# Gate operations issued one by one behind the evacuations of up, and unread products of TensorE ahead of the first loads

## The chip, the cores and the metric

The kernel runs on one NeuronCore of a Trainium2 chip. The metric is the device time of one execution in microseconds (us), as a median of several runs. The engines are TensorE (PE, with its weight loads listed apart as PEld), VectorE (DVE), ScalarE (ACT), GpSimd (POOL) and SyncE (SP, which only issues DMAs here). Each engine works through a queue of its own in order.

## The reference

A block of cross attention and a quantised feed-forward block, over 4096 tokens of 512 features.

```python
x = x + _L0_xattn_ref(_layernorm(x, axis=-1), ctx_1024, L0_xattn_Wq, L0_xattn_Wkv)
x = x + _L0_ffn_ref(_layernorm(x, axis=-1), L0_ffn_w_gate, L0_ffn_w_up, L0_ffn_w_down)
```

The attention is `softmax(hWq (cWk)^T / sqrt(512)) cWv` with 128 context rows for each of the two batches. In the feed-forward block every activation tensor is rounded to 16-bit integers with one scale for the whole tensor:

```python
x = act_qdq(x)
up = act_qdq(x @ lpbq_dequant(w_up).T)
gate = act_qdq(x @ lpbq_dequant(w_gate).T)
sig = fixed_qdq_u16(jax.nn.sigmoid(gate))
gate = act_qdq(gate * sig)
o = act_qdq(gate * up)
return o @ lpbq_dequant(w_down).T
```

`act_qdq` needs the largest magnitude of its tensor before the first element can be rounded. So the stages of the kernel stand one behind the other.

## The kernel before, in words

There are four stages, each over eight groups of 512 tokens.

**Attention** (0 to about 157 us of the profiled execution). The context `c_sb` and the matrix `wq_sb` are turned by TensorE (lines 400 and 408) into PSUM tiles of two banks, which come from a pool `ps_t` with two buffers. VectorE copies the turned context to `cT` (line 401), ScalarE copies the turned matrix to `wqT` (line 409). From `cT` come the keys (`pk`, line 417, copied to `kT` by ScalarE in line 424), from `wqT` and `kT` the product `pg` (line 431), which becomes `kTG` (line 438, then line 445 on VectorE, which takes a mean `pm` off). Then each group g has its scores `sc` (line 351), softmax (`e`, line 364), turned weights (`pe`, copied to `eT` in line 466), values `po` (line 478, added to x in line 479), the second layernorm (lines 497 to 508) and the turn of `h` into `hT`. `front(g)` works ahead on the transposes of x (line 311) and its statistics (line 338 on VectorE; for group 1 lines 321, 324, 326 and 333 with ScalarE). In between, the gate's weights are dequantised, turned and split (`split_weights`, lines 180 to 215). The stage ends in one number, the largest `h` (`a_h`), and TensorE has nothing of the gate stage to do before it is known.

**Gate** (to 434.9 us), **up** (to about 701 us), **down** (to the end). In the up stage (loop from line 857) step c makes half of a tile of up: sixteen products q and eight products e of TensorE (lines 621 and 627), ScalarE's evacuation of q (line 878) and VectorE's subtraction of e (line 879). q and e have two buffers each, so the products of step c + 2 wait for the evacuation of step c. Beside this, ScalarE makes the gelu of one gate tile in three operations of 128x2048 elements: line 769 to integers, line 772 the sigmoid, line 773 the sigmoid as 16-bit integers. They are called G1, G2 and G3 below. It also makes |up| for a bound (line 819, called b below). VectorE makes p = gi * sq (line 812), the bound's product (line 820) and the largest |up| (line 180). SP loads gate tiles (line 755) and stores up (line 893) and p (line 813).

The order on each engine is not that of the source. A scheduler places each instruction by its own estimate of when its inputs are ready. `in_order(a, b)` forces b behind a on one engine; `advance(steps, n)` runs n steps of a generator.

Of the kernel before, what the change touches and what calls it, by code (L numbers as in the profile page):

```python
# [49 lines left out]
F32 = mybir.dt.float32  # L50
# [6 lines left out]
AF = mybir.ActivationFunctionType  # L57
# [6 lines left out]
P = 128  # L64
# [12 lines left out]
def tile_xattn_ffn(  # L77
# [11 lines left out]
    nc = tc.nc  # L89
    B, S, D = x.shape  # L90
# [5 lines left out]
    NQ = 4  # L96
    NK = NF // NQ
    TG = 512
# [11 lines left out]
    ident = const.tile([P, P], F32, name="ident")  # L110
# [8 lines left out]
    order = [(t, k) for t in reversed(range(NG)) for k in range(NK)]  # L119
    gate_d = dram.tile([NG * NK, P, NQ, TG], F32, name="gate_d")  # L120
    NH = 2 * NG * NK
# [47 lines left out]
    def in_order(*instructions):  # L169

        for one, behind in zip(instructions, instructions[1:]):
            tc.add_manual_dep(
                behind.ins,
                one.ins.name,
                mybir.DependencyInfo(mybir.DependencyClass.NoSync, mybir.DependencyReason.DATA),
                reason="order of issue",
            )
# [63 lines left out]
    def advance(steps, n):  # L241
        for _ in range(n):
            next(steps, None)
# [29 lines left out]
    with ExitStack() as c0:  # L273
# [3 lines left out]
        with ExitStack() as c1:  # L277
# [5 lines left out]
            ps_s = c1.enter_context(tc.tile_pool(name="ps_s", bufs=2, space=PSUM))  # L283
# [91 lines left out]
            with tc.tile_pool(name="prep0", bufs=1, side="right") as p0:  # L375
# [16 lines left out]
                xts[1] = load_x(1)  # L392
                advance(its[1], 1)

                cT = p0.tile([P, ND, B * KL], F32, name="cT")
                pt = two_banks("ct")
                pt4 = pt.rearrange("p (c b k) -> p c b k", c=ND, b=B)
                for b in range(B):
                    for c in range(ND):
                        nc.tensor.transpose(pt4[:, c, b, :], c_sb[:, b, ts(c, P)], ident)  # L400
                nc.vector.tensor_copy(cT.rearrange("p c k -> p (c k)"), pt)
                wqT = p0.tile([P, ND, D], F32, name="wqT")
                for m in range(0, ND, 2):
                    pt = two_banks(f"wqt_{m}")
                    pt4 = pt.rearrange("p (c m k) -> p c m k", c=ND, m=2)
                    for i in range(2):
                        for c in range(ND):
                            nc.tensor.transpose(pt4[:, c, i, :], wq_sb[:, m + i, ts(c, P)], ident)
                    nc.scalar.copy(wqT[:, :, ts(m // 2, 2 * P)], pt.rearrange("p (c k) -> p c k", c=ND))
                first = front(0)  # L410
                advance(its[0], 3)
# [330 lines left out]
    with ExitStack() as c3:  # L742
# [10 lines left out]
        def load_gate(j, queue=nc.sync):  # L753
            gt = gp2.tile([P, NQ, TG], F32, tag="gt", name=f"gt_{j}")
            queue.dma_start(out=gt, in_=gate_d[j])
            return gt
# [5 lines left out]
        s_g16 = const.tile([P, 1], F32, name="s_g16")  # L762
        nc.vector.tensor_scalar(s_g16, s_g, 1.0 / 65536.0, None, ALU.mult)

        def gelu_like(pool, gt, shape, name, behind=None):

            sq = pool.tile([P] + shape, U16, tag="sq", name=f"sq_{name}")
            gi = pool.tile([P] + shape, I16, tag="gi", name=f"gi_{name}")
            begun = nc.scalar.activation(gi, gt, AF.Copy, scale=r_g)
            if behind is not None:  # L770
                in_order(behind, begun)
            nc.scalar.activation(gt, gi, AF.Sigmoid, scale=s_g)
            nc.scalar.activation(sq, gt, AF.Copy, scale=65536.0)
            return gi, sq


        gi, sq = gelu_like(const, top_g, [1], "top")
# [16 lines left out]

        wd, ready, made_p = [], [], []

        def next_gelu(behind):

            j = len(ready)
            if j < len(order):  # L800
                ready.append(gelu_like(wk3, gts.pop(0), [NQ, TG], j, behind))
                if j + 2 < len(order):
                    gts.append(load_gate(j + 2))

        def next_p():
            j = len(made_p)
# [45 lines left out]
        LAST = len(order) - 1  # L852


        more_gelu = (1, NH // 4 + 1, 3 * NH // 8 + 1, 5 * NH // 8 + 1)
        more_p = (NH // 3 + 1, NH // 2 + 3)
        for j, (t, k) in enumerate(order):
            if k == 0:
                parts = groups.pop(t)
                if t + 1 < NG and t > 0:  # L860
                    groups[t - 1] = load_group(t - 1)
                if t == 0:
                    first_wd = homes[1].tile([P, 3, ND, TG], F32R, tag="parts", name="first_wd")
                    first_wd = first_wd.rearrange("p s c (k d) -> p (s c k d)", k=1).rearrange(
                        "p (f s d) -> p f s d", f=NE, s=3
                    )
                    load_down(range(NE), slice(0, 2))
            u4 = tiles_u[j % NK]
            for h in range(2):
                c = 2 * j + h  # L870
                both = slice(2 * h, 2 * h + 2)
                wu2 = [wu[NQ * k + 2 * h + i] for i in range(2)]
                if c + 1 < NH:
                    q = ps_m.tile([P, 2, TG], F32, tag="q", name=f"q_u{c}")
                    e = ps_m.tile([P, 2, TG], F32, tag="e", name=f"e_u{c}")
                    for i in range(2):
                        project(wu2[i], parts, q[:, i, :], e[:, i, :])
                    evacuated = nc.scalar.activation(u4[:, both, :], q, AF.Copy, scale=1.0 + 1.0 / BASE)  # L878
                    less = nc.vector.tensor_tensor(u4[:, both, :], u4[:, both, :], e, ALU.subtract)  # L879
                    if c + 2 == NH:  # L880
                        in_order(row_known, less)
                else:
                    for i in range(2):
                        v = u4[:, 2 + i, :]
                        q = ps_m.tile([P, 2, TG], F32, tag="q", name=f"q_u{c}_{i}")[:, 0, :]
                        e = ps_m.tile([P, 2, TG], F32, tag="e", name=f"e_u{c}_{i}")[:, 0, :]
                        last_product = project(wu2[i], parts, q, e)
                        nc.scalar.activation(v, q, AF.Copy, scale=1.0 + 1.0 / BASE)
                        nc.vector.tensor_tensor(v, v, e, ALU.subtract)
                        abs_max(umax[:, LAST + 1 + i : LAST + 2 + i], v)  # L890
                if t == 0 and k == 0 and h == 1:
                    load_down(range(NE, NE + NQ), slice(0, 2))
                stored = nc.sync.dma_start(out=up_d[c], in_=u4[:, both, :])
                if h == 0 or c in more_gelu:

                    next_gelu(evacuated if c > 3 else None)
                if h == 0 or c in more_p:
                    next_p()
                pi = kept_p[j % NK]
                if c + 3 < NH:  # L900
                    bound(c, u4[:, both, :], pi[:, both, :])
                elif c + 3 == NH:
                    with tc.high_priority():
                        bound(c, u4[:, both, :], pi[:, both, :])
                        row_known, (ub, pb) = fetch_best()
            if j < LAST:
                abs_max(umax[:, j : j + 1], u4, AX.XY)
            else:
                abs_max(umax[:, j : j + 1], u4[:, :2, :], AX.XY)
# [329 lines left out]
```

## Time and profile before

| | us |
|---|---|
| median of 3 runs | 981.71 (978.31 to 982.92) |
| the profiled execution, its own time | 981.48 |
| its span on the core | 979.7 |
| TensorE busy | 947.5 |
| VectorE busy | 812.5 |
| ScalarE busy | 548.7 |
| first product of the gate stage starts at | 159.49 |
| first product of the up stage starts at | 434.87 |
| first product of the down stage starts at | 711.95 |

The times in the rows below are counted from the start of the span. A row of the timeline is: start, duration, engine, line, operation, output<-input, shapes, count, and in brackets the idle time before it with what ended it. A plain fp32 product of the attention stage, and an unread one, is recorded twice, so sixteen products `sc` stand there as x32. Transposes, and the products of the other three stages, are recorded once. TensorE's clock is given in tenths of full speed, or as a fraction in the table of stretches.

### The profile page before, as it was taken

Reading aid. Unit: us, or ns where it says so; the run is one execution under the profiler, and the core shown is the slowest. Engines: PE = TensorE matmul, PEld = TensorE weight load, DVE = VectorE, ACT = ScalarE, POOL = GpSimd, SP = SyncE. Lnnn points to the kernel's source line nnn. Section 1 sums busy time; section 2 is a strip of 40 time slices with the busy share of each in tenths; the row PEclk is TensorE's granted clock in tenths of the full one; section 3 lists DMA queues with packets and bytes.
Section 4 is the critical chain, followed back from the end, with each engine's and each line's share of the span. In section 5 each row is a group of like instructions: output and inputs, shape, how many; then the busy total and the mean of one; then the engine's idle time right before and its main releaser. Section 6 shows DMA issues by size and latency. Waiting matters only on the chain. (4 is left out here: it accounts for less than half of the span.)

```text
span 979.7 us, 11777 instructions
## 1 busy us (share of the span) xinstructions
PE 947.5 (97%) x4356; PEld 763.4 (78%) x4356; DVE 812.5 (83%) x1013; ACT 548.7 (56%) x668; POOL 77.9 (8%) x62
## 2 busy tenths in 40 slices
PE   6998889999999999999999999999989999999998
PEld 6775656888888888877888888877668888888886
DVE  4979779899899998537988989879799999878882
ACT  3477689323323323229999999795455445353531
POOL 0101111000000000000000000000101221222221
PEclk9999899999999999999999999999999999999999
DMA  9675545967878855897988989979785677656710
GB/s 359 247 280 199 178 178 236 414 266 302 322 311 313 321 194 174 279 409 251 370 315 306 403 285 374 379 270 377 292 319 177 210 256 256 211 152 230 259 64 32
DMA packets 103595, 263.72 MB, mean 269 GB/s; under 512 B 6064, under 2 KB 46000, under 8 KB 94832
## 3 DMA queue, kind: packets, MB, share of 16 engines
q1 hardware_dynamic: 102496, 259.02, 71.7%
q0 software_dynamic: 512, 2.88, 0.9%
q10 hardware_dynamic: 528, 1.05, 0.3%
q8 instruction: 34, 0.56, 0.2%
q14 instruction: 25, 0.20, 0.1%
HBM read 136.05 MB, written 126.88 MB: 268 GB/s over the span
## 5 line engine op out<-in xcount | busy, mean ns | idle before, releaser
L621 PE MATMUL q_g<-parts_g,wg 128*128 128x512 f32 x768 | 193.1, 391 | 0.9 <-ACT parts_g L644 0.9
L621 PEld LDWEIGHTS q_g<-parts_g,wg 128*128 128x128 f32 x768 | 143.4, 188 | 31.2 <-ACT parts_g L644 2.0
L712 ACT ACTIVATE g<-q_g 128x512 f32<-128x512 f32 x96 | 57.3, 598 | 166.0 <-PE q_g L621 155.5
L621 PE MATMUL q_u<-parts_u,wu 128*128 128x512 f32 x576 | 142.7, 390 | 2.6 <-ACT u L878 2.6
L621 PEld LDWEIGHTS q_u<-parts_u,wu 128*128 128x128 f32 x576 | 107.9, 188 | 26.1 <-ACT u L878 3.7
L1040 PE MATMUL yq<-wd,o_parts 128*128 128x512 f32 x512 | 121.4, 389 | 0.5 <-ACT o_parts L1029 0.5
L1040 PEld LDWEIGHTS yq<-wd,o_parts 128*128 128x128 f32 x512 | 96.0, 188 | 20.9 <-ACT o_parts L1029 0.9
L627 PE MATMUL e_g<-parts_g,wg 128*128 128x512 f32 x384 | 103.3, 390 | 0.0
L713 DVE CUSTOM_DVE_ANT_0 g<-g,e_g 128x512 f32<-128x512 f32 x96 | 65.0, 682 | 36.6 <-PE e_g L627 33.4
L627 PEld LDWEIGHTS e_g<-parts_g,wg 128*128 128x128 f32 x384 | 72.0, 188 | 15.1
L1053 ACT ACTIVATE yqs<-yq,q_o 128x512 f32<-128x512 f32 x32 | 22.0, 686 | 101.5 <-PE yq L1040 100.4
L627 PE MATMUL e_u<-parts_u,wu 128*128 128x512 f32 x288 | 77.0, 389 | 0.0
L1029 ACT CAST o_parts<-sa 128x1536 fp32r<-128x1536 int16 (+3 forms) x39 | 48.4, 1243 | 44.5 <-DVE sa L1026 44.3
L1032 DVE SCALAR_TENSOR_TENSOR o_parts<-sa,oi 128x1536 fp32r<-128x1536 int16 (+2 forms) x33 | 60.0, 1819 | 14.8 <-PE ye L1048 14.8
L879 DVE TENSOR_TENSOR u<-u,e_u 128x1024 f32<-128x1024 f32 x47 | 57.0, 1218 | 18.2 <-ACT u L878 18.0
L1057 POOL TENSOR_TENSOR qx<-yqs,x 128x512 f32<-128x512 f32 x28 | 54.0, 1928 | 211.8 <-ACT yqs L1053 140.9
L820 DVE CUSTOM_DVE_ANT_0 ua<-ua,pi 128x1024 f32<-128x1024 f32 x46 | 56.0, 1220 | 12.8 <-ACT ua L819 12.6
L1040 PE MATMUL yq<-first_wd,o_parts 128*128 128x512 f32 x256 | 63.7, 390 | 2.0 <-ACTq L1104 1.2
L1028 DVE SCALAR_TENSOR_TENSOR o_parts<-sa,oi 128x1536 fp32r<-128x1536 int16 (+3 forms) x39 | 57.4, 1472 | 9.7 <-PE yq L1040 7.0
L1048 PE MATMUL ye<-wd,o_parts 128*128 128x512 f32 x256 | 63.2, 389 | 0.0
L627 PEld LDWEIGHTS e_u<-parts_u,wu 128*128 128x128 f32 x288 | 54.1, 188 | 11.3
L878 ACT ACTIVATE u<-q_u 128x1024 f32<-128x1024 f32 x47 | 47.7, 1014 | 23.4 <-PE q_u L621 23.2
(215 smaller groups left out, 1578.2 us busy)
## 6 DMA issues: line engine op xcount, KB each, us to landing
gate_d<-g SPq DMA_DIRECT2D x24, 1024.0 KB, 7.4
up_d<-u SPq DMA_DIRECT2D x48, 512.0 KB, 8.4
gt<-gate_d SPq DMA_DIRECT2D x22, 1024.0 KB, 7.1
u<-up_d SPq DMA_DIRECT2D x21, 1024.0 KB, 9.2
parts_d<-parts_g SPq DMA_DIRECT2D x6, 3072.0 KB, 13.3
parts_u<-parts_d SPq DMA_DIRECT2D x6, 3072.0 KB, 14.3
p_d<-pi SPq DMA_DIRECT2D x24, 512.0 KB, 10.6
p<-p_d SPq DMA_DIRECT2D x84, 128.0 KB, 2.9
```

The lines of the kernel that those rows point to most:

```text
L621: nc.tensor.matmul(q, lhsT=w[:, s, c, :], rhs=parts[:, s, c, :], start=(c + s == 0), stop=(c + s == ND))
L627: made = nc.tensor.matmul(e, lhsT=w[:, 2, c, :], rhs=parts[:, 2, c, :], start=(c == 0), stop=(c == ND - 1))
L712: evacuated = nc.scalar.activation(g4[:, i, :], q, AF.Copy, scale=1.0 + 1.0 / BASE)
L713: subtracted = nc.vector.tensor_tensor_reduce(g4[:, i, :], g4[:, i, :], e, 1.0, LOWEST, ALU.subtract, ALU.max, gtop[:, m : m + 1])
L820: nc.vector.tensor_tensor_reduce(ua, ua, pi, 1.0, 0.0, ALU.mult, ALU.max, pumax[:, c : c + 1])
L879: less = nc.vector.tensor_tensor(u4[:, both, :], u4[:, both, :], e, ALU.subtract)
L1028: made.append(nc.vector.scalar_tensor_tensor(parts[1][:, c], sa[:, c], -BASE, oi[:, c], ALU.mult, ALU.add))
L1029: return made, nc.scalar.copy(parts[0][:, c], sa[:, c])
L1032: return nc.vector.scalar_tensor_tensor(parts[2][:, c], sa[:, c], BASE + 1.0, oi[:, c], ALU.mult, ALU.subtract)
L1040: nc.tensor.matmul(q, lhsT=parts[s][:, f, :], rhs=wd[f][:, s, :], start=(f + s == 0), stop=(f + s == NF))
L1048: nc.tensor.matmul(e, lhsT=parts[2][:, f, :], rhs=wd[f][:, 2, :], start=(f == 0), stop=(f == NF - 1))
L1057: nc.gpsimd.tensor_tensor(qx, qs, x1[:, m % NU, :], ALU.add)
```

## The change

Two parts.

**In front of the first loads.** Eighteen products `ident x ident` into an unread PSUM tile are put at the head of TensorE's queue, and twelve more between the turn of the context and the turn of `wq_sb`. They are ordinary fp32 products, not transposes. The unread tile takes one buffer of `ps_s`.

**In the up stage.** `gelu_like` becomes a generator of three steps, one for each of G1, G2 and G3. Step c of the loop takes two of them when h is 0 and one when h is 1, and one more at the twelve values of c in `more_gelu`. From c = 4 on, each operation taken is placed behind the evacuation of step c. Before, all three were made at once, on every even c and at four odd ones, and only G1 was placed behind the evacuation. Gate tile j + 2 is loaded when the steps of tile j are used up.

```diff
+                unread = ps_s.tile([P, D], F32, tag="tr", name="unread_0")[:, :P]
+
+                def idle_first(n):
+                    return [nc.tensor.matmul(unread, lhsT=ident, rhs=ident, start=True, stop=True) for _ in range(n)]
+
+                idle_first(18)
                 cT = p0.tile([P, ND, B * KL], F32, name="cT")
...
                 for b in range(B):
                     for c in range(ND):
-                        nc.tensor.transpose(pt4[:, c, b, :], c_sb[:, b, ts(c, P)], ident)
+                        turned = nc.tensor.transpose(pt4[:, c, b, :], c_sb[:, b, ts(c, P)], ident)
+                in_order(turned, *(waits := idle_first(12)))
                 nc.vector.tensor_copy(cT.rearrange("p c k -> p (c k)"), pt)
...
-                            nc.tensor.transpose(pt4[:, c, i, :], wq_sb[:, m + i, ts(c, P)], ident)
+                            turned = nc.tensor.transpose(pt4[:, c, i, :], wq_sb[:, m + i, ts(c, P)], ident)
+                            if m + i + c == 0:
+                                in_order(waits[-1], turned)
...
-        def gelu_like(pool, gt, shape, name, behind=None):
+        def gelu_steps(pool, gt, shape, name, made):
...
-            begun = nc.scalar.activation(gi, gt, AF.Copy, scale=r_g)
-            if behind is not None:
-                in_order(behind, begun)
-            nc.scalar.activation(gt, gi, AF.Sigmoid, scale=s_g)
-            nc.scalar.activation(sq, gt, AF.Copy, scale=65536.0)
-            return gi, sq
+            yield nc.scalar.activation(gi, gt, AF.Copy, scale=r_g)
+            yield nc.scalar.activation(gt, gi, AF.Sigmoid, scale=s_g)
+            last = nc.scalar.activation(sq, gt, AF.Copy, scale=65536.0)
+            made.append((gi, sq))
+            yield last
+
+        def gelu_like(*args):
+            made = []
+            advance(gelu_steps(*args, made), 3)
+            return made[0]
...
-        def next_gelu(behind):
-
-            j = len(ready)
-            if j < len(order):
-                ready.append(gelu_like(wk3, gts.pop(0), [NQ, TG], j, behind))
+        def all_gelu():
+            for j in range(len(order)):
+                yield from gelu_steps(wk3, gts.pop(0), [NQ, TG], j, ready)
                 if j + 2 < len(order):
                     gts.append(load_gate(j + 2))
+
+        gelu = all_gelu()
...
-        more_gelu = (1, NH // 4 + 1, 3 * NH // 8 + 1, 5 * NH // 8 + 1)
+        more_gelu = [0, 1, 2] + [c + d for c in (NH // 4 + 1, 3 * NH // 8 + 1, 5 * NH // 8 + 1) for d in (0, 2, 4)]
...
-                if h == 0 or c in more_gelu:
-
-                    next_gelu(evacuated if c > 3 else None)
+                n = 2 - h + (c in more_gelu)
+                steps = [step for step in (next(gelu, None) for _ in range(n)) if step is not None]
+                if c > 3:
+                    in_order(evacuated, *steps)
```

**The order in which the instructions are issued**, as both kernels are built. On VectorE, from the start to the subtraction of line 445 (lines of the kernel before; g0 to g3 are the four blocks of gate weights, x0 to x3 the groups of x):

```
before: cT | x0: 338 x4, 339 x4, 340 | g0: 180 193 195 197 199 | g1: 180 | 324 | g1: 193 195 197 |
        g0: 208 | g1: 199 | g0: 210 | 333 | x2: 338 | g0: 213 | x2: 339 338 | 445 x4
after:  x0: 338 x4, 339 x4, 340 | cT | g0: 180 193 195 197 199 | g1: 180 193 195 197 | x2: 338 |
        g1: 199 | 324 | x2: the rest of 338 and 339 | x3: 338 x3, 339 x3 | g0: 208 210 | 333 340 |
        g0: 213 | g2: 180 | x3: 338 339 340, g2: 193 195 | g2: 197 | 445 x4
```

On ScalarE before `pg`, the copies of the two halves of `kT` (line 424) stand, after the change, the first behind three of the four operations of line 321, and the second behind the fourth of them and the first operation of line 326. That last one waits for line 324 on VectorE. Before, both copies stood ahead of line 326.

On ScalarE in the up stage, what stands between the evacuation of step c and that of step c + 1:

```
 c   before              after        |  c   before              after
 6   G1 G2 b G3          G1 G2 b      | 24   G2 b G3 G1          G3 G1 b G2
 7   -                   G3 b         | 25   G2 b G3             G3 b
 8   G1 b G2 b G3        b            | 26   G1                  -
 ... (c = 0 to 5 alike)               | 34   b b                 G1 G2 b G3 G1
15   G1 b G2             G1 b G2      | 35   G1 b G2             G2 b G3 G1
16   G3 G1 b G2          G3 G1 b G2   | 36   G3 G1 b G2          G2 b G3 G1
17   G3 b                G3 G1 b G2   | 37   G3 G1 b G2          G2 b G3
18   G1                  G3 G1 b G2   | 38   G3 G1 b G2          -
19   G2 b G3 G1 b G2     G3 b         | 39   G3 b                b b
20   G3 b                -            | 40   -                   G1 G2 b G3
21   -                   b G1 b G2    |
22   b b G1              G3 G1 b G2   |
23   G2 b G3 G1          G3 G1 b G2   |
```

SP issues the same DMAs. Some gate tile loads stand one to three places later in its queue, behind a store of p or of up.

## Prediction

> **What bounds the kernel now.** I read the page first, then the chain of waits of TensorE, then the timeline of the two places that the change touches.
>
> ```profile
> span 979.7 us, 11777 instructions
> PE 947.5 (97%) x4356; PEld 763.4 (78%) x4356; DVE 812.5 (83%) x1013; ACT 548.7 (56%) x668; POOL 77.9 (8%) x62
> ```
>
> TensorE is busy for 97% of the span, so most of the kernel cannot be shortened by another order. Its share is lower only in the attention stage. There the stretches of 10 us show TensorE at 6.4 to 10.0 and VectorE at 5.2 to 10.0 between 50 and 150 us: a stage of waits in a ring, not of one full engine. It ends in `a_h` at 156.88 us, which everything later waits for. So a delay of that number moves the end by as much.
>
> The head of the attention stage, from the timeline:
>
> ```profile
> 8.00 1.22 DVE L401 COPY cT<-ct 128x1024 f32<-128x1024 f32 x1 [8.00 <-PE ct L400]
> ...
> 8.78 3.67 PE L408 MATMUL wqt<-ident,wq_sb 128*128 128x128 f32 x16 [0.81 <-DMA wq_sb<-in_L_xattn_Wq]
> ...
> 12.82 1.29 DVE L338 BATCH_NORM_STATS2 st<-xt 128x6 f32<-128x512 f32 x2 [3.60 <-DMA xt<-in_x]
> ...
> 34.71 1.40 DVE L445 TENSOR_TENSOR kTG<-kTG,pm 128x256 f32<-128x256 f32 x4
> ...
> 35.86 3.73 PE L351 MATMUL sc<-kTG,xT 128*128 128x128 f32 x32
> ...
> 48.66 0.68 DVE L466 COPY eT<-pe 128x512 f32<-128x512 f32 x1
> ```
>
> The reader is to see the order: `cT` is copied at 8.00, before the x rows land at 12.82; the first scores start at 35.86, right behind line 445; `eT` of group 0 follows at 48.66.
>
> In the up stage TensorE waits for ScalarE's evacuation only:
>
> ```profile
> PE q_u L621 <- ACT u L878: 3.5, 3, 1.7
> ```
>
> ```profile
> 646.68 1.00 ACT L878 ACTIVATE u<-q_u 128x1024 f32<-128x1024 f32 x1
> 647.58 1.90 ACT L773 ACTIVATE sq<-gt 128x2048 uint16<-128x2048 f32 x1
> 649.38 1.99 ACT L769 ACTIVATE gi<-gt,r_g 128x2048 int16<-128x2048 f32 x1
> 651.27 1.05 ACT L819 ACTIVATE ua<-u 128x1024 f32<-128x1024 f32 x1
> 652.23 2.00 ACT L772 ACTIVATE gt<-gi,s_g 128x2048 f32<-128x2048 int16 x1
> 654.12 1.00 ACT L878 ACTIVATE u<-q_u 128x1024 f32<-128x1024 f32 x1
> ...
> 655.18 2.34 PE L621 MATMUL q_u<-parts_u,wu 128*128 128x512 f32 x9 [0.93 <-ACT u L878]
> ```
>
> A step with three gelu operations takes ScalarE 7.44 us from evacuation to evacuation (654.12 less 646.68), while a step of TensorE takes 5.44 (two times 2.72, from the starts of the rows). Several such steps in a row push the evacuation later until TensorE stands.
>
> **The change at the head of the attention stage.** The scheduler answers the thirty products by moving the copy of `cT` on VectorE behind the statistics of x0. That counts more than the products.
>
> *The products.* Thirty-two records of `sc` take 3.73 us, so 0.117 a record and 0.23 a product at full clock. The turn of the context takes 1.94 for 8 records, so about 0.24 a record at the start, 0.48 a product. Eighteen products from about 1.8 us (the identity is ready at 1.67) take 4.2 to 8.6 us; twelve take 2.8 to 5.8. If the clock rises at about 7 us, the context is turned by 9.6 and the twelve end near 12.4, not at 7.97 as the context's turn did. I cost both lots at nothing: VectorE has not reached the copy by then. Without that cover they would cost up to 4 us; a gain is bounded by the 1.8 us that full clock takes off the turn of `wq_sb` (3.67 to 1.85).
>
> *The copy.* The x0 rows land at 12.82, their statistics run to 15.85 (rows of lines 338 to 340), the copy takes 1.22: `cT` is there at 17.07, not at 9.22. Two things wait. The second half of the turn of `wq_sb` needs the buffer of the context's turn, so TensorE stands from about 13.4 to 17.1. And `pk` follows at 18.1 or later, not at 12.25.
>
> *The clock.* In this trace the clock halves after such a gap: TensorE did only transposes and waits from 103 to 109 us, and the granted clock was 0.50 from about 109.4 to 116.3; four records of `po` took 3.78 us there and 1.88 elsewhere. The Trainium skill, "TensorE: Matmul & The Clock Gate", Part 1, says that the clock falls after one idle window of about 3.4 us and that busy work must fill a window before it rises. It speaks against this change, since the gap of 3.7 us undoes the warming. With the clock kept, `pk` ends at 18.1 + 1.8 + 1.9 + 5.35 (8 records, 16 transposes of x0, 24 records) = 27.2; by the rule about 3.2 later, at 30.4. Before it was 21.87. I take 30.4. The sum is the same by both, since ScalarE's copy behind it waits for VectorE until 31 in either case:
>
> *The queues behind it.* On ScalarE the second half of `kT` stands behind the first operation of line 326, which waits for line 324 on VectorE. VectorE from 17.07, by the durations in the timeline: block g0 to 23.4, lines 180 to 197 of g1 to 27.5, a statistic of x2 0.65, line 199 1.75, then line 324 at about 30.0. So line 326 runs to 31.0 and `kT` is whole at 31.6. `pg` needs it and two buffers that ScalarE still has to empty of turned gate weights; it starts near 33.9 (before 25.32) and takes 7.2. `pm` ends near 43.2 (before 34.3).
>
> VectorE meanwhile works through what the new order puts ahead of line 445: statistics of x2 and x3 to 34.2, line 208 to 35.5, line 210 to 37.3, line 213 to 39.3, line 180 of g2 to 41.0, statistics and small operations to 42.5, line 197 to 44.2. Line 445 starts at 44.2, and scores at about 45.4 (before 35.86), 9.5 late. Some of that work stood behind the scores before, so the lateness must be read at a point with equal work done: `eT`. Scores with one product `pvs` between end at 50.1, line 359 and the exponentials at 52.9; TensorE first does the five products `pvs` (10 records of 0.47) to 54.8 and turns of gate weights to 56.6; `eT` starts at 57.2, 8.6 late, and the scores of group 1 at 57.0 instead of 47.72, **9.3 late**.
>
> *Does it come back?* One round from scores to scores is 3.7 scores, 0.9 for line 359 and 360, 2.9 for line 508, 1.9 exponentials, 1.9 copies of xT, 2.0 turns of h: 13.3. The rounds from 57 to 98 us took 13.1, 14.2 and 13.9. Nothing in this ring got shorter, so I carry 9.3 to `a_h` and to the end.
>
> **The change in the up stage.** Starts follow each other by 0.90 (evacuation), 1.90 (G1, G2), 1.80 (G3), 0.95 (b). I sum these over the order listed with the change, less 5.44 a step, from a lag of 0.2. An evacuation may lag 5.3 behind its products (the one at 654.12 had its products at 647.9, lagged 6.2 and cost 0.93). *Removed:* the waits at 655.18 and 662.62; the rows show 0.93 and 1.68, and the starts of TensorE show 1.1 + 2.0 = 3.1 against an even 5.44. *Kept:* the one at 463.21, since c = 0 to 5 are alike. *Added:* c = 16 to 18 make three operations each, so the lag is 0.4, 2.4, 4.4, 6.4: 1.1 over. From c = 21: 1.4, 3.4, 5.4, then 7.3: 0.1 + 2.0 over. From c = 34, with four operations: 4.1, 6.1, 7.3, 5.4: 0.8 + 2.0 + 0.1. Together 6.0, so the stage gets **2.9 longer**. What is queued behind the late evacuations: VectorE's line 879 and with it lines 820 and 812, and SP's stores and gate loads behind those; a gate load took 7.1 us to land, and its G1 may wait once more in a dense run. Nothing in the trace shows that wait beyond one of 1.2 (before G1 at 486.64); I bound it at 0 to 3 and take 0, since the dense runs before showed none. If the scheduler's groups are loosened by waits instead, the gain is at most the 3.1.
>
> **Sum.** 9.3 + 2.9 = 12.2 on the profiled execution's 981.5 gives 993.7. The median of the runs, 981.71, is 0.2 from that execution, so the time is measured against either.
>
> **The rivals.**
>
> *A, it comes back.* VectorE has 21.7 us idle between 50 and 150 us (100 less 78.3 busy). If that idle time, and not the ring, is what separates the rounds, the late head is made up before `a_h`: 981.5 + 2.9 = 984.4, within 0.5% and so not slower. It decides where the scores of group 7 start: at 131.82 before; A if under 134. For it: x2 and x3 have their statistics early. Against: so they had before, and the rounds are as long as the ring's sum.
>
> *B, the steps do what they say.* The runs of three dissolve on the chip, because G1 waits for its tile and the lag never builds up. Then the 3.1 are gained: 981.5 + 9.3 - 3.1 = 987.7. A and B together give 978.4, and 975.0 if the half clock at 109 (6.8 us, costing 3.4) does not return.
>
> *C, more.* A second stretch at half clock of 6.8 us costs 3.4 and a waiting gate load 3: about 1000.
>
> *D, the unread products bring what they can.* This needs `cT` early, which VectorE's queue excludes; it is within A.
>
> **How the numbers follow.** A difference of 0.5% (4.9 us) is about what a measurement of this kernel can tell from none. The likeliest case 0.56 (991 to 997), B alone 0.15 (985 to 990), A alone 0.11 (981 to 987), A with B 0.08 (975 to 979), C 0.10. Over 986.6 lie the first, C and 0.13 of B: 0.79. Below 976.8 about half of A with B, and a share for a trace misread: 0.07. Within: 0.14. The range goes from 983 to 1000, leaving out A with B, a third of A and some of C.
>
> **What would show it.** Right, if line 401 starts near 15.9, TensorE stands near 13 to 17, line 445 starts near 44, `eT` near 57, `a_h` near 166, and the waits of `q_u` for line 878 sum to about 6 at c = 21, 26 to 27 and 38 to 40. Wrong, if `a_h` is before 160, or if those waits are under 2.

## The result, and the profile after

The changed kernel takes 994.59 us as a median of four runs (993.38 to 996.42); the kernel before, run beside it, 980.31 (978.31 to 982.92). The ratio is 1.014, 95% interval 1.0122 to 1.0158: slower by 14.3 us, and the prediction of 993.7 is 0.9 below it. The profiled execution took 995.7 us.

From the page of the changed kernel, span and engines:

```profile
span 993.9 us, 11902 instructions
PE 956.4 (96%) x4416; PEld 772.5 (78%) x4416; DVE 811.0 (82%) x1013; ACT 550.3 (55%) x668; POOL 80.0 (8%) x62
```

VectorE and ScalarE work as long as before (812.5 and 548.7). TensorE's 8.9 us more come from the unread products (6.63 and 2.84 in the next fence). They put off the turn of the context from 6.03 to 8.19 and the turn of `wq_sb` from 8.78 to 11.74, but VectorE comes to the copy of `cT` only at 15.72. So what the span grew by, 14.2 us, is to be looked for in waits behind them.

They lie in two places. The product that makes `a_h` (`rows_h`, line 151) starts at 163.69 (before 156.55), the first of up at 442.20 (before 434.87), and from there the up stage, up to the start of its last evacuation, takes 272.15 us instead of 265.25. So 7.1 us were lost ahead of `a_h` and 6.9 in the up stage.

The head of the attention stage in the timeline of the changed kernel. Line 410 is line 401 of before, 417 is 408, 428 is 417, 442 is 431, 456 is 445, 477 is 466:

```profile
1.72 6.63 PE L400 MATMUL unread<-ident 128*128 128x128 f32 x36 [1.72 <-POOL ident masks.py:199]
8.19 1.04 PE L408 MATMUL ct<-ident,c_sb 128*128 128x128 f32 x8
9.06 2.84 PE L400 MATMUL unread<-ident 128*128 128x128 f32 x24
11.74 1.04 PE L417 MATMUL wqt<-ident,wq_sb 128*128 128x128 f32 x8
...
15.72 1.22 DVE L410 COPY cT<-ct 128x1024 f32<-128x1024 f32 x1
...
17.00 1.97 PE L417 MATMUL wqt<-ident,wq_sb 128*128 128x128 f32 x8 [4.22 <-DVE cT L410]
...
18.76 2.67 PE L428 MATMUL pk<-cT,wk_sb 128*128 128x256 f32 x8
...
33.14 7.17 PE L442 MATMUL pg<-kT,wqT 128*128 128x256 f32 x32
...
42.78 1.41 DVE L456 TENSOR_TENSOR kTG<-kTG,pm 128x256 f32<-128x256 f32 x4
...
43.69 0.83 PE L351 MATMUL sc<-kTG,xT 128*128 128x128 f32 x6
...
54.56 3.74 PE L351 MATMUL sc<-kTG,xT 128*128 128x128 f32 x32
54.76 0.69 DVE L477 COPY eT<-pe 128x512 f32<-128x512 f32 x1 [3.01 <-PE pe L475]
```

The turn of the context is done by 9.23, but `cT` is copied only at 15.72, behind the statistics of x0. TensorE stands 4.22 us for it. The turn of eight records takes 1.04 us ahead of that gap and 1.97 behind it: the clock that the unread products had raised is lost (the granted clock is 0.50 from 18 to 20 us). The scores start at 43.69, 7.8 late, and those of group 1 at 54.56, 6.8 late.

The up stage, from the chain of waits (us in total, times, longest) and the timeline of the changed kernel; lines 632 and 895 are 621 and 878 of before:

```profile
PE q_u L632 <- ACT u L895: 9.2, 7, 1.7
```

```profile
465.04 2.10 PE L632 MATMUL q_u<-parts_g,wu 128*128 128x512 f32 x8 [0.80 <-ACT u L895]
472.49 2.11 PE L632 MATMUL q_u<-parts_g,wu 128*128 128x512 f32 x8 [1.51 <-ACT u L895]
...
560.81 2.11 PE L632 MATMUL q_u<-parts_u,wu 128*128 128x512 f32 x8 [0.99 <-ACT u L895]
...
589.98 2.11 PE L632 MATMUL q_u<-parts_u,wu 128*128 128x512 f32 x8 [1.65 <-ACT u L895]
597.43 2.12 PE L632 MATMUL q_u<-parts_u,wu 128*128 128x512 f32 x8 [1.72 <-ACT u L895]
...
658.40 2.12 PE L632 MATMUL q_u<-parts_u,wu 128*128 128x512 f32 x8 [0.81 <-ACT u L895]
665.84 2.11 PE L632 MATMUL q_u<-parts_u,wu 128*128 128x512 f32 x8 [1.69 <-ACT u L895]
```

Three waits, at c = 5, 40 and 41, have become seven, at c = 4, 5, 21, 26, 27, 38 and 39; c is the step whose products wait. Each costs a little more than its bracket, since eight products behind it take 2.1 us and not 1.98.

### The profile page after: what moved, and what is told of

Same layout as the page of the kernel before. It is cut to its first block, busy times and chain, and to the rows that moved or that the text cites. A ratio compares the mean times of both kernels' runs of the same rounds, so it can differ in the third digit from the quotient of the medians.

```text
span 993.9 us, 11902 instructions
## 1 busy us (share of the span) xinstructions
PE 956.4 (96%) x4416; PEld 772.5 (78%) x4416; DVE 811.0 (82%) x1013; ACT 550.3 (55%) x668; POOL 80.0 (8%) x62
## 5 line engine op out<-in xcount | busy, mean ns | idle before, releaser
L828 DVE SCALAR_TENSOR_TENSOR pi<-gi,k_p,sq 128x2048 int16<-128x2048 int16 x24 | 56.3, 2348 | 4.2 <-ACT sq L783 4.1
## 6 DMA issues: line engine op xcount, KB each, us to landing
parts_d<-parts_g SPq DMA_DIRECT2D x6, 3072.0 KB, 14.3
```

The lines of the kernel that those rows point to most:

```text
L828: nc.vector.scalar_tensor_tensor(pi, gi, k_p, sq, ALU.mult, ALU.mult)
```

## The experiments

Of the twelve kernels, nine take the head apart and three the up stage. The theory: in the head, the changed order of VectorE's queue is the loss and the products are not; in the up stage, the loss is the dense runs of ScalarE's steps. The rivals are written with each run.

### The two parts alone

`e1_front` has the first part of the change only, `e2_up` the second only.

> The kernel before with the thirty unread products alone; the up stage keeps the order of before. My theory (the two parts add up; the head costs 7.1 us at a_h and nothing of it comes back): a_h about 163.7, the end +7 us (about 987), and TensorE waits for line 878's evacuation only where before waited, 3.5 us in all. Also to be read here: the first gate tile of the up stage landed 1.9 us later in the changed kernel, measured from TensorE's first up product. If that belongs to the shifted head (other traffic at that moment), it shows here and adds 2 (about 989). Rival (the head's loss is made up later, and the up stage carries the whole difference): less than +3.

> The kernel before with the gelu steps alone; the head keeps the order of before. ScalarE's order in the up stage is line for line that of the changed kernel. My theory as the prediction had it (sums of ScalarE's operations alone): +2.9, with the waits of q_u at c = 21, 26 to 27 and 38 to 40. What the changed kernel's trace showed: 1.8 us more at c = 26, and 1.9 more at c = 4 and 5 behind the first gate tile. If both belong to the up part itself: +7. If the first gate tile's lateness belongs to the head: +5.

Measured: `e1_front` 988.74 against 980.91, 1.0081 (1.0063 to 1.0098). `e2_up` 985.28, 1.0044 (1.0027 to 1.0061). The two losses, 7.8 and 4.4, add to 12.2 of the change's 14.3. In `e1_front` `a_h`'s product starts 6.3 later than before and the up stage is 0.6 longer. (The trace of `e1_front` has less half clock near 110 us than that of before; against `e2_up`, whose head is that of before and whose clock there is the same as `e1_front`'s, it is 7.1 later.) In `e2_up` the up stage takes 270.21, 5.0 longer. The chain of waits of `e2_up`:

```profile
PE q_u L621 <- ACT u L884: 7.7, 6, 1.7
```

Six waits, at c = 5, 21, 26, 27, 38 and 39. The waits at c = 21 to 39 therefore belong to the up part. The first gate tile does not: at c = 4 and 5 TensorE waits 0.85 us in `e2_up`, 1.50 in `e1_front`, and 2.31 in the changed kernel with both. Neither part alone makes all of that. The excess is about the 2.1 us by which the two losses fall short of the whole, but the intervals of the three ratios would also cover it.

### Which queue of the head loses the time

Four kernels change the place of the copy of `cT` or of the copies of `kT`. `e3_copy_first` is `e1_front` with the copy of `cT` held ahead of x0's statistics, as before:

```diff
-                        nc.vector.bn_stats(st, xt[:, j, :])
+                        begun = nc.vector.bn_stats(st, xt[:, j, :])
+                        if copied is not None and j == 0:
+                            in_order(copied, begun)
...
-                first = front(0)
+                first = front(0, copied)
```

`e4_copy_last` is the reverse: the kernel before, no products, with that copy held behind them (`in_order(known, copied)`, where `known` is line 340).

> The unread products stay, and VectorE's copy of cT is held ahead of the first statistic of x0; up stage as before. My theory (the displaced copy is the whole loss, the products cost nothing by themselves): the loss of 7 us goes; the copy starts near 9.3, the turn of wq_sb runs from 11.7 to 13.6 at full clock, pk begins near 13.6 against 12.25 before but runs its first 8 records in 1.9 instead of 2.7; the end within 2 us of the kernel before. Rival (the products themselves occupy TensorE when it is needed): still 4 us or more behind the kernel before. Rival (a warm clock pays, once the copy is in place): 1.5 us or more ahead of it.

> No unread products; VectorE's copy of cT is held behind the last operation of x0's statistics, where the changed kernel has it; up stage as before. My theory (VectorE's order alone carries the loss): cT whole at about 17, the second half of the turn of wq_sb waits for it, and the end is +5 to +8 us. Rival (the products and the clock that falls after them carry it): within 2 us of the kernel before.

Measured: `e3_copy_first` 989.93, 1.0092 (1.0072 to 1.0111), no better than `e1_front`. `e4_copy_last` 986.58, 1.0065 (1.0046 to 1.0084). So the late copy, with no products, costs about 5.7 us, but putting it back gains nothing. (No hold here is pure: the scheduler places other instructions anew around it, and the trace of `e4_copy_last` has another order than before on TensorE, VectorE and ScalarE.) My theory that the displaced copy is the whole loss fell here. The timeline of `e3_copy_first` (its line 412 is the copy of `cT`, 430 `pk`, 437 the copy of `kT`, 444 `pg`, 458 is line 445 of before):

```profile
9.83 1.23 DVE L412 COPY cT<-ct 128x1024 f32<-128x1024 f32 x1 [9.83 <-PE ct L410]
...
17.54 5.35 PE L430 MATMUL pk<-cT,wk_sb 128*128 128x256 f32 x24
...
27.82 0.72 ACT L326 ACTIVATE unread_x<-xt,row_x 128x512 f32<-128x512 f32 x1 [1.63 <-DVE row_x L324]
...
29.25 0.56 ACT L437 COPY kT<-pk 128x512 f32<-128x512 f32 x1
...
32.90 8.20 PE L444 MATMUL pg<-kT,wqT 128*128 128x256 f32 x32
...
43.03 1.42 DVE L458 TENSOR_TENSOR kTG<-kTG,pm 128x256 f32<-128x256 f32 x4 [2.09 <-PE pm L456]
```

`pk` is done at 22.9, about as before (21.87). But the second copy of `kT` stands behind line 326 on ScalarE, which waits until 27.82 for line 324 on VectorE. `pg` starts at 32.90 all the same, within 0.3 of the changed kernel.

So `e6_keys_first` and `e5_both_held` also hold the copies of `kT` ahead of x1's sums and squares. `e6_keys_first` leaves the copy of `cT` late, `e5_both_held` puts it first as well:

```diff
-                    nc.scalar.copy(kT[:, m : m + 2, :], pk)
+                    keys.append(nc.scalar.copy(kT[:, m : m + 2, :], pk))
...
+                        in_order(keys[0], summed)
...
+                        in_order(keys[1], squared)
```

> Run e3 with ScalarE's order of before as well: the first copy of kT is held ahead of the four sums over x1 (line 321), the second ahead of the four squares (line 326). Why: with the copy of cT first, the head still lost 8 us, though pk ended at 22.9 (before 21.9); there ScalarE emptied the second half of pk at 29.25 only, behind two squares that wait for VectorE's line 324. My theory now (two queues were re-ordered, VectorE's and ScalarE's, and each alone makes kT late): kT is whole at 23 to 25, the scores of group 0 start at 37 to 38, and the end is within 2.5 us of the kernel before. Rival (something else in the head, such as loads that land later, carries e3's loss): still 5 us or more behind.

> The thirty products with ScalarE's order held as in e5, but VectorE's copy of cT left where the changed kernel has it, behind x0's statistics. By my theory kT's second copy follows pk at once, at 28.4 instead of 30.8; VectorE's place of the copy remains, so the end is 4 to 6 us behind the kernel before (without the hold, e1 was 7.8 behind; with the copy late and no products, e4 was 5.7 behind). Rival (ScalarE's order carries all): within 2 us of the kernel before. Rival (VectorE's place alone counts): as e1, 7 to 8.

Measured: `e5_both_held` 986.78 against 980.6, 1.0064 (1.0048 to 1.008). `e6_keys_first` 988.5, 1.008 (1.0065 to 1.0095). In `e5_both_held` `kT` is whole at 24.6, but TensorE's next instruction ahead of `pg`, a turn of gate weights, waits for line 199 of g0, which ends on VectorE at 26.9. The turns behind that gap of 5.31 us run slow (eight take 1.91 us, and 1.15 in `e6_keys_first`), and `pg` starts at 31.75. In `e6_keys_first` `kT` is whole at 29.1, `pg` starts at 31.48, and still line 445 starts at 42.81, as in the changed kernel: VectorE has other work ahead of it.

`e9_eighteen` drops the twelve products and holds the copy of `cT` and both copies of `kT` first. `e10_three_held` is `e5_both_held` with one hold more on VectorE, line 199 of g0 ahead of line 180 of g1:

```diff
-        abs_max(s, w3)
+        began = abs_max(s, w3)
+        if name == "g1":
+            in_order(held[0], began)
...
+        if name == "g0":
+            held.append(back)
```

`e11_eighteen_held` is `e10_three_held` without the twelve products.

> Head only: the eighteen products ahead of the context's turn stay, the twelve behind it are left out; VectorE's copy of cT is held first, and both copies of kT ahead of x1's sums on ScalarE; up stage as before. The products that are read then run at full clock with nothing in their way: the turn of wq_sb from 9.7 to 11.4 (before 12.3), pk ends near 20.5 (before 21.9), kT whole near 21.1 (before 22.9). Theory A (the start of pg is what counts): 1.5 to 2 us ahead of the kernel before. Theory B (VectorE, which was busy without a gap until line 445 at 34.7, takes over as the bound): within 1 us of it.

> Run e5 (thirty products, copy of cT first, ScalarE's order held) with one more hold on VectorE: line 199 of gate block g0 ahead of line 180 of g1, as in before. Why: in e3, e5 and e9 VectorE has line 180 of g1 first, stands for its load until 23.1 to 23.5, and line 199 of g0 ends at 26.5 to 26.9 (before 23.4); in TensorE's queue the turned gate weights wt_g, which need it, are ahead of pg, so pg starts at 30.5 to 32.9 though kT was whole at 21.2 to 24.6. My theory now (what costs is the order of three queues around the copy, not the products): pg starts at 26 to 28, the scores of group 0 at 37 to 39, the end within 3 us of the kernel before, and well ahead of e5 (6.2 behind). Rival (it is the products' own time or later loads): 5 us or more behind.

> The same holds as e10 with the eighteen products alone (the twelve left out). If the warm clock is worth anything at the end, this shows it: pk ends near 20.6 (before 21.9). Theory A (the start of pg counts): 1 to 2 us ahead of the kernel before. Theory B (x1's sums on ScalarE, which wait for the rows of x1 at 20 to 21.6, and VectorE's queue up to line 445 set the time): within 1.5 us of it, either side.

Measured: `e9_eighteen` 986.87, 1.0063 (1.0051 to 1.0075). `e10_three_held` 988.43 against 980.94, 1.0088 (1.0062 to 1.0114). `e11_eighteen_held` 986.7, 1.0066 (1.0042 to 1.009). None comes back to the time before.

Part of that is not the head's. In the traces of `e5_both_held`, `e9_eighteen`, `e10_three_held` and `e11_eighteen_held` the up stage is 2.5 to 3.7 us longer than before, though ScalarE has the order of before there. One gate tile lands 8.1 to 8.7 us after its issue instead of 6.2, G1 waits 0.7 to 1.3 us for it in the middle of the dense run, and TensorE's wait at c = 41 grows from 1.68 us to between 2.5 and 3.1. From the timeline of `e9_eighteen` (781 is G1) and its chain of waits:

```profile
660.70 2.00 ACT L781 ACTIVATE gi<-gt,r_g 128x2048 int16<-128x2048 f32 x1 [1.27 <-DMA gt<-gate_d]
```

```profile
PE q_u L633 <- ACT u L890: 4.8, 3, 3.1
```

Why that tile is late in these four is open.

The rest is lost in the head. The timeline of `e10_three_held` (line 452 is `pg`, 466 is line 445 of before, 361 the scores):

```profile
25.86 7.17 PE L452 MATMUL pg<-kT,wqT 128*128 128x256 f32 x32
...
36.67 1.74 DVE L180 TENSOR_REDUCE ws_g<-w_g 128x48 f32<-128x1536 f32 x1
...
38.93 1.39 DVE L466 TENSOR_TENSOR kTG<-kTG,pm 128x256 f32<-128x256 f32 x4
...
39.39 0.84 PE L361 MATMUL sc<-kTG,xT 128*128 128x128 f32 x4 [3.55 <-DVE kTG L466]
```

Here `pg` starts at 25.86, 0.5 from before, and `pm` is done at 35.0. Line 445 nevertheless starts at 38.93, behind line 180 of g2 and statistics of x, which stood behind it before. TensorE waits 3.55 us for it. Here the hold moved the loss to the next place that was not held.

### All queues held

`e13_all_held` settles it. It is the kernel before with the thirty products, and every engine's queue of the attention stage is held in the order of the kernel before. A wrapper notes each instruction as it is made, and the recorded order is then imposed; `runs` holds it as first numbers and lengths:

```diff
+    in_order(*[made[first + i] for first, n in runs for i in range(n)])
```

The products are the only difference that is left: in the traces, every engine has the attention stage's instructions in the order of before, apart from the products.

> The kernel before plus the thirty unread products, with every queue of the attention stage (TensorE, VectorE, ScalarE, GpSimd and SP's DMAs) held in the order that it has in before; the products are the only difference in any queue. Why: e10 had kT, wt_g and pg where before has them (pg at 25.9), and still lost 7 us, because VectorE had a statistic of x2 that waited for its load and line 180 of g2 in its queue ahead of line 445, which came at 38.9 instead of 34.7. So hold after hold the loss moved to the next place in which the order differs. My theory (the loss of the head is the order of the queues, above all VectorE's, and the products themselves cost next to nothing): pk ends at 21.9 to 22.9 (before 21.9), line 445 at 34.5 to 35.5, a_h at 156 to 158, the end within 1.5 us of the kernel before. Rival (the products cost the time, by what they occupy or by the clock): a_h at 160 or later, the end 4 us or more behind. Rival (a warm clock gains once nothing is moved): 1.5 us or more ahead.

Measured: 981.5 (22 runs) against 980.65 (27 runs), 1.0004 (0.9993 to 1.0015): no difference beyond that interval. Its timeline (all wrapped instructions have line 125):

```profile
8.25 1.23 DVE L125 COPY cT<-ct 128x1024 f32<-128x1024 f32 x1 [8.25 <-PE ct L125]
...
10.73 1.91 PE L125 MATMUL wqt<-ident,wq_sb 128*128 128x128 f32 x16
...
15.95 5.34 PE L125 MATMUL pk<-cT,wk_sb 128*128 128x256 f32 x24
...
21.50 0.63 ACT L125 ACTIVATE unread_x<-xt 128x512 f32<-128x512 f32 x1 [3.03 <-DMA xt<-in_x]
...
23.96 0.56 ACT L125 COPY kT<-pk 128x512 f32<-128x512 f32 x1
```

The products do what they can: the turn of `wq_sb` takes 1.91 us instead of 3.67, with no gap behind it. It brings nothing, because the second copy of `kT` stands in ScalarE's queue behind x1's sums, and those wait for x1's rows.

The attention stage of these kernels side by side, and how long their up stage takes, in us of their profiled executions:

| kernel | line 445 | scores 0 | scores 1 | `a_h`'s product | scores 1 to it | up stage | ratio |
|---|---|---|---|---|---|---|---|
| before | 34.71 | 35.86 | 47.72 | 156.55 | 108.83 | 265.3 | |
| `e13_all_held` | 37.30 | 38.74 | 50.59 | 158.47 | 107.88 | 265.4 | 1.0004 |
| `e4_copy_last` | 38.94 | 40.38 | 51.80 | 160.71 | 108.91 | 265.9 | 1.0065 |
| `e11_eighteen_held` | 38.32 | 38.79 | 50.52 | 159.13 | 108.61 | 267.7 | 1.0066 |
| `e9_eighteen` | 40.47 | 41.91 | 53.15 | 159.21 | 106.06 | 268.1 | 1.0063 |
| `e5_both_held` | 41.30 | 42.74 | 54.16 | 163.09 | 108.93 | 268.0 | 1.0064 |
| `e10_three_held` | 38.93 | 39.39 | 54.43 | 163.38 | 108.95 | 269.0 | 1.0088 |
| `e6_keys_first` | 42.81 | 43.28 | 54.48 | 163.46 | 108.98 | 265.1 | 1.008 |
| after | 42.78 | 43.69 | 54.56 | 163.69 | 109.13 | 272.2 | |
| `e1_front` | 42.94 | 43.85 | 54.72 | 162.83 | 108.11 | 265.9 | 1.0081 |
| `e3_copy_first` | 43.03 | 44.47 | 55.89 | 164.89 | 109.00 | 265.7 | 1.0092 |

Times ahead of the scores of group 1 can be compared from trace to trace: `e2_up`, `e7_spread` and `e12_one_less` have the attention stage of before, instruction for instruction, and their scores 1 start at 47.91, 47.70 and 47.86. From there to `a_h`'s product the same stage took 108.83, 107.82, 107.45 and 105.96 us in these four traces, with the granted clock between 100 and 150 us at 0.93, 0.97, 0.97 and 1.00. All the kernels of the table lie in about that range (106.1 to 109.1), and the lowest, `e9_eighteen`, had full clock there. So what is late at the scores of group 1 stays late. Most holds win back little there, but `e11_eighteen_held` is only 2.8 us late, against 6.8 for the changed kernel; the other half of its 5.8 us is in the up stage. `e10_three_held` shows that the scores of group 0 alone do not decide.

The profiled execution of `e13_all_held` took 983.65, 2.2 above its median. In it x1's rows landed at 21.50, and its first sum started then; in the traces of before, `e1_front`, `e2_up` and the changed kernel that sum starts at 19.9 to 20.1. That points to something the products do besides the order. The second block of gate weights (line 187), issued at 8.7 to 9.1 in all fourteen traces, lands at 23.1 to 23.5 in the nine with products and at 21.9 to 22.1 in the five without. In each of the nine a DMA packet of 16 KB, of the kind that the profile calls `instruction`, comes at 16.8 to 20.9 us, among these loads, and from the load then on its way they land 1.1 to 1.6 us late. In the five it comes at 26.3 to 29.6. That TensorE's longer queue calls for it earlier is argued from these times; no run separates it. Over the 22 runs of `e13_all_held` it and the products together cost between -0.7 and 1.5 us.

### The up stage

`e7_spread` asks whether single steps could be placed so that no run is dense. It has the up part only, with the extra steps spread evenly and each step held behind its evacuation and ahead of the next one. The edit against the changed kernel, without its first part:

```diff
-        more_gelu = [0, 1, 2] + [c + d for c in (NH // 4 + 1, 3 * NH // 8 + 1, 5 * NH // 8 + 1) for d in (0, 2, 4)]
+        more_gelu = [0, 1, 3, 9, 13, 17, 21, 25, 29, 33, 37]
...
-                    in_order(evacuated, *steps)
+                    in_order(*(behind + [evacuated] if c + 1 < NH else behind), *steps)
+                behind = steps
```

> Up part only: each step of the gelu is held behind its evacuation and ahead of the next one, and the eleven extra steps are spread (c = 0, 1, 3, 9, 13 and so on to 37), so that no two evacuations have three gelu operations between them more than once in a row; the head as before. My sums of ScalarE's operations give no lag over 5.3 anywhere. Theory (runs of three operations are what stops TensorE): the waits for the evacuation go from 3.5 us to under 1, and the end is 3 to 4.5 us ahead of the kernel before. Rival (held in this order, ScalarE stands at a gate tile that has not landed, with the evacuation behind it, since such loads took up to 13 us): new waits of TensorE of 3 us or more, the end no better than before.

Measured: 987.84, 1.0074 (1.0055 to 1.0094), no better than `e2_up` (1.0044, 1.0027 to 1.0061). The rival came true. From the chain of waits of `e7_spread`, and its timeline:

```profile
ACT gi L770 <- DMA gt<-gate_d: 10.8, 7, 3.7
PE q_u L621 <- ACT u L884: 6.9, 7, 3.6
```

```profile
664.04 2.00 ACT L770 ACTIVATE gi<-gt,r_g 128x2048 int16<-128x2048 f32 x1 [3.75 <-DMA gt<-gate_d]
665.95 1.00 ACT L884 ACTIVATE u<-q_u 128x1024 f32<-128x1024 f32 x1
...
667.01 3.50 PE L621 MATMUL q_u<-parts_u,wu 128*128 128x512 f32 x8 [3.60 <-ACT u L884]
```

G1 waits 3.75 us for its gate tile, the evacuation stands behind it, and TensorE waits 3.60 for that. There are two gate buffers, and a load is issued only when a tile's steps are used up, so an even spread leaves it no time.

`e12_one_less` goes the other way: the kernel before, with one extra gate tile taken out of the dense run that ended in its two late waits.

```diff
-        more_gelu = (1, NH // 4 + 1, 3 * NH // 8 + 1, 5 * NH // 8 + 1)
+        more_gelu = (1, 13, 19)
```

> The kernel before without the fourth extra gelu tile (c = 31 taken out of more_gelu); ScalarE's order is that of before up to c = 35, and behind it no two steps of three operations follow each other. Theory (dense runs stop TensorE, and nothing else does there): the waits at 655 and 662 go, 3.2 us ahead of the kernel before. Rival (gate tiles that land late, as in e7, take their place, or the tail of the stage gets longer because the last tiles are late): no gain, or a loss of 1 to 3.

Measured: 977.06 (12 runs) against 980.94, 0.996 (0.9948 to 0.9971): faster than both kernels by more than its interval. The up stage takes 261.92 us, 3.3 less than before. Its chain of waits:

```profile
PE q_u L621 <- ACT u L878: 0.9, 1, 0.9
```

The waits at c = 40 and 41 (655.18 and 662.62 before) are gone and the one at c = 5 is left.

## Why the prediction was right, step by step

*The copy.* Right: line 401 predicted at 15.85, measured at 15.72; TensorE predicted to stand 3.7, measured 4.22. What the step leaves out is that the copy is not the loss but one of its places: `e4_copy_last` loses 5.7 with it late and no products, `e3_copy_first` 9.0 with it early.

*The products at nothing.* Right within the interval of `e13_all_held`, -0.7 to 1.5 us. The twelve end at 11.90 (predicted 12.4). That the loads behind them would land later, the prediction does not have.

*The clock.* The rule that the prediction took from the Trainium skill held here: after the gap of 4.22 the second turn ran at half speed (1.97 against 1.04, granted clock 0.50 from 18 to 20 us). `pk` ends at 28.36, 2.0 earlier than the 30.4 taken: half clock cost 1.7 (0.93 at that turn, and 0.78 at eight records of `pk`, 2.67 against 1.89 in `e3_copy_first`), where 3.2 was taken. As the prediction said, this had no weight: the operation of line 326 ahead of the copy of `kT` waited for line 324 until 29.92 (predicted 30.0), and `kT` was whole at 31.2 (predicted 31.6).

*The queues behind it.* `pg` 33.14 for 33.9. Line 445 at 42.78 for 44.2: here the sum was too high by 1.4. The mis-sized term is VectorE's work ahead of line 445, where the operations of lines 208 to 213 and 197 ended 0.9 to 1.3 earlier than summed. The other 1.0 is spread over the steps from there to the scores of group 1, 0.3 or 0.4 at a time (line 445 to the scores 0.9 for 1.2, the ten records of `pvs` 4.3 for 4.7). So the head was late by 6.8 at the scores of group 1, not by 9.3.

*Carrying it.* Right: 6.8 there, 7.1 at `a_h`. Rival A is refuted: the scores of group 7 start at 138.34, where A needed less than 134, and in no kernel of the table is the lateness made up beyond what the clock of its execution gives.

*The up stage.* The removed waits, 3.1, were right: `e12_one_less`, which only removes that run, gets 3.3 back. Those added at c = 21, 27, 38 and 39 came where the sum put them, at 1.3, 2.0, 1.1 and 2.0 (idle time and slower restart; predicted 1.1, 2.0, 0.8 and 2.0). So the runs do not dissolve, and rival B is refuted too. Two terms were too small. At c = 26 the prediction has 0.1 and the trace 1.9. At c = 4 and 5 it keeps the wait that was there (1.1), since the order there is alike, and the trace has 3.1. ScalarE's first G1 waits there for the store of the last gate tile (`gate_d<-g` in the row below), which lands 10.2 us after its issue instead of 8.0. In the fourteen traces that store takes 7.6 to 10.2 us, so it is open whether the 2.0 belong to the kernel or to the execution. With both terms the stage is 6.9 longer, not 2.9. The late gate load, which the prediction bounds "at 0 to 3" and takes at 0, fell inside its bound ahead of c = 26. From the timeline of the changed kernel (781 is G1, 835 is b, 836 the bound's product, 896 line 879, 828 line 812):

```profile
452.46 2.00 ACT L781 ACTIVATE gi<-gt,r_g 128x2048 int16<-128x2048 f32 x1 [1.57 <-DMA gate_d<-g]
```

```profile
566.52 2.35 DVE L828 SCALAR_TENSOR_TENSOR pi<-gi,k_p,sq 128x2048 int16<-128x2048 int16 x1
568.39 2.00 ACT L781 ACTIVATE gi<-gt,r_g 128x2048 int16<-128x2048 f32 x1 [0.69 <-DMA gt<-gate_d]
568.79 1.22 DVE L836 CUSTOM_DVE_ANT_0 ua<-ua,pi 128x1024 f32<-128x1024 f32 x1
569.93 1.22 DVE L896 TENSOR_TENSOR u<-u,e_u 128x1024 f32<-128x1024 f32 x1
571.18 1.06 ACT L835 ACTIVATE ua<-u 128x1024 f32<-128x1024 f32 x1 [0.79 <-DVE u L896]
```

In the second fence the reader is to see two pauses of ScalarE in the middle of a dense run, where the sum had none: 0.69 for a gate tile, and 0.79 for a subtraction that stood behind p and the bound's product on VectorE. Together 1.5 of the 1.8 missing at c = 26. `e2_up` has the same two pauses, 0.83 and 0.65, and the same wait at c = 26 (1.66), so they belong to the up part. That both are its cause is argued from these windows; no run separates the two.

*The sum.* 9.3 + 2.9 = 12.2 was measured as 7.1 + 6.9 = 14.0, with 0.2 from the rest of the span. That the total lies 0.9 from the median is luck in part: the head was summed 2.2 too high and the up stage 4.0 too low, and the profiled execution is 1.1 above its median.

## What to carry to other kernels

Where a scheduler orders the queues, instructions added to one engine can reorder the others: compare every queue before and after, and price what now stands ahead of the operation that the next stage waits for. Holding one to three displaced instructions back in place left most of the loss, at the next one or, by a late load, in another stage; only holding all of them showed what the added products were worth, which was nothing. Compare the stages of a trace one by one before a loss in the total is put down to the stage that was edited. In a run of work that is denser than the engine beside it, count operations for each step and remove one (0.996 here) before splitting them finer, and count the loads that refill its buffers in the same sum.

## What the runs showed of the hardware

- A short gap of TensorE can cost the clock too. In the up stage, eight products took 2.10 to 2.12 us behind gaps of 0.80 to 1.72 (the changed kernel), and 3.32 to 3.66 behind gaps of 2.49 to 3.60, against 1.98 with no gap (`e5_both_held`, `e7_spread`, `e9_eighteen`, `e10_three_held`, `e11_eighteen_held`). Behind the gap of 3.07 in `e9_eighteen` the granted clock was 0.50 from 668 to 670 us. The shortest such gap, 2.49 us, is well under the window of about 3.4 us that the Trainium skill gives in "TensorE: Matmul & The Clock Gate", Part 1. That page also calls the window free-running; no run here shows whether that is why.
- Transposes follow the clock as well: sixteen took 3.67 us in the kernel before and 1.91 behind the unread products (`e13_all_held`). The granted clock of the profile reads 1.00 there in both, so at the start of these kernels only the durations show the slow clock.
- A gate tile of 1 MB landed 6.0 to 7.3 us after its issue in twelve of the 22 loads of the up stage before, and 8.9 to 12.6 in the ten that are the first or second behind a 3 MB load of `parts_u`. In the changed kernel, the two behind the load of `parts_u` at 552.21, issued at 555.14 and 562.58, took 13.2 and 11.9.
- The stretch at half clock near 110 us differs between executions of the same instructions: in the four traces that share the attention stage of before, the granted clock between 100 and 150 us was 0.93, 0.97, 0.97 and 1.00, and the way from the scores of group 1 to `a_h` up to 2.9 us longer for it.
